# Loading the rows of x1 earlier, spreading the attention gates, and moving one absolute value in a fused two-layer convolution kernel

## The chip, the cores and the metric

The kernel runs on one core of a Trainium2 chip. The metric is the device time of one execution in microseconds. Kernels are compared by the median of their executions. The profile is of one execution. Engines carry the names of the profile: PE is TensorE (PEld its weight loads), DVE is VectorE, ACT is ScalarE, POOL is GpSimd, SP is SyncE, which here only issues transfers. DMAs are issued by SP, ACT and POOL.

## What is computed

The input is 32 images of 96 channels and 56 by 56 pixels, in float32. Two layers follow one another.

Layer 0 is an inverted bottleneck with squeeze and excitation. Its weights pass through `fake_quant` (8 bits).

```python
h = silu(bn(conv1x1(x, w1)))            # 96 -> 576 channels
h = silu(bn(depthwise3x3(h, w2)))
s = sigmoid(W2 @ silu(W1 @ mean(h) + b1) + b2)
x1 = x + bn(conv1x1(h * s, w3))         # 576 -> 96
```

Layer 1 attends x1 with a channel gate and a spatial gate, and then deforms it.

```python
mag = abs(rfft2(x1)); ca = channel_gate(mag)             # one number per channel
sa  = spatial_gate(mean(x1), l2(x1), resize(mean(mag)))  # one number per pixel
y = x1 * ca * sa
aux = concat(y, coordinates, resize(mean(abs(rfft2(y)))))
offset = conv3x3(aux)                   # 18 channels
gate = sigmoid(conv1x1(relu(conv3x3(aux))))
y_base = conv3x3(y)
y_def = deformed 3x3 convolution of y: 9 taps, each sampled bilinearly at its offset
z = (1 - gate) * y_base + gate * y_def
out = relu(batch_norm(z over all images and pixels) + x1)
```

## The kernel before, in words

`layers()` computes x1 and z of all images and stores them in DRAM; `normalise()` then reads both back and applies the batch norm. A branch for offsets that reach too far isn't taken with these inputs.

An image is cut into seven bands of eight rows. The main loop in `layers()` runs over the 224 bands of all images, and a band has two halves of seven tiles of 4 by 4 pixels for each of its two tile rows. Beside the sampling of band n of image b, three streams run ahead. They are Python generators, which issue a few instructions at each step and then yield. `pump()` advances them once per slot; an image has 70 slots, so one is about 4.2 us.

- `first` is `hidden()` of image b + 2: the expansion (L166 on PE, L170 on ACT), the depthwise taps (L257 and L259 on DVE), and SiLU (L219 on ACT) with the store to `h2d` on ACT's queue.
- `second` is `attend()` of image b + 1: the projection, whose operands `hq` come from `h2d` (L307 on SP, L323 on PE, L325 on ACT), with the residual added on POOL (L443) and x1 stored in DRAM (`x1d`, L444); then the magnitudes of the transform (`dft_mag`, x loaded by SP at L351, L376 to L400), the channel gate `ca`, the spatial gate `sa` (sigmoid L273 and L274), its store `sad` (L538 on POOL), and a second transform of x1 gated by sa (L356 on POOL), which gives the row `fq`.
- `find(n + 2)` is `offsets()` for the band two ahead, advanced once per slot within the band: the joint 3x3 convolution (L582 on PE), its hidden part (L603 on ACT), the offsets copied out of PSUM (`at`, L630, two on DVE), the base convolution (L606 and L614 on ACT, L611 on PE, L616 on DVE), the offsets to DRAM (`od`, L634 on POOL's queue) and back, spread over partitions (`ht`, L646 on SP). Then come the bilinear weights 1 - |offset - position|: the absolute value (Abs, L649) and Relu (L650), both on ACT, and a store to DRAM (`hd`, L653 on ACT's queue).

For each half band, `prepare()` loads column and row weights from hd (`wc` and `wr`, L664 and L665 on SP, four loads of 252 KB) and `weights()` multiplies them (L671 on DVE). `block_channels()` copies the pixels out (L682 on POOL), transposes them (L686 on PE, L688 on ACT), `sample_tiles()` multiplies them with the weights (L700 on PE, copied out by L704 on ACT to `v`), `pack()` moves channels onto the free partitions (L711, three on ACT), and `deform()` runs the deformed convolution (`pd`, L719 on PE). `gate_of()` gives the gate (L727, L729), `combine()` z (L745 to L748 on DVE).

The padded image of y, `yp`, is one buffer in SBUF whose rows are overwritten for the next image when the sampling of this one has left them. `refill(b, upto)` does that after each band: `load_rows()` loads x1 rows into it (L561 on SP) and the matching rows of sa, repeated over the channels, into `sab` (L563 on POOL's queue), and four slots later `attend_rows()` multiplies in place by ca and sab (L569 on DVE). It starts with the first call after sa exists. `load_freq()` puts the row fq in place (L573 on SP).

The list `later` holds actions that are due at a slot. At band 5 of an image (`turn`) the streams are drained, `flush()` runs everything in `later` at once, and the streams start anew for the next image.

What sets the order: SP is in a region whose schedule is manual, so it issues in the order in which the program was written. On the other engines a scheduler orders the instructions within their dependences. Pools with several buffers decide how far a load can run ahead; `hq` has eight, and an x1 group of seven rows needs five or six of them.

Of the kernel before, what the change touches and what calls it, by code (L numbers as in the profile page):

```python
# [9 lines left out]
AF = mybir.ActivationFunctionType  # L10
ALU = mybir.AluOpType
AX = mybir.AxisListType
PSUM = bass.MemoryType.PSUM
DRAM = bass.MemoryType.DRAM
# [6 lines left out]
RB = 8  # L21
# [277 lines left out]
def project_loads(nc, p, x, h2d, q):  # L299

    half, n0 = divmod(q * EW, HB)
    terms = [(u, ch, slice(0, 128)) for u, (ch, hf) in enumerate(UNITS) if hf == half]
    terms.append((4, 4, slice(64 * half, 64 * half + 64)))
    rows = []
    for u, ch, ps in terms:
        hq = p["hq"].tile([128, EW], FP, name="hq")
        nc.sync.dma_start(hq[ps], h2d[u, ps, n0 : n0 + EW])  # L307
        rows.append((ch, ps, hq))
    return rows
# [113 lines left out]
def attend(tc, p, b, x, h2d, pooled, x1, given=False):  # L423
# [5 lines left out]
    nc = tc.nc  # L429
    w = p["w"]  # L430
    if not given:
        rows = [project_loads(nc, p, x, h2d, 0)]
        yield from squeeze(nc, p, pooled)
        rows.append(project_loads(nc, p, x, h2d, 1))
        for _ in range(2):
            yield
        for q in range(H // ER):
            xr = residual_load(nc, p, x, q)
            o = project(nc, p, rows.pop(0))
            yield  # L440
            if q + 2 < H // ER:
                rows.append(project_loads(nc, p, x, h2d, q + 2))
            nc.gpsimd.tensor_tensor(o, o, xr, ALU.add)  # L443
            nc.gpsimd.dma_start(x1[:, q * EW : (q + 1) * EW], o)  # L444
            yield
    yield


# [43 lines left out]
    ca = p["ca"].tile([C, 1], FP, name="ca")  # L492
# [28 lines left out]
    r = p["sp"].tile([H, 3, W], FP, name="r")  # L521
# [5 lines left out]
    sa = p["sp"].tile([H, W], FP, name="sa")  # L527
# [6 lines left out]
    sa = p["sp"].tile([2 * H, W], FP, name="sa2")  # L534
# [20 lines left out]
    p["fq", b] = fqd  # L555


def load_rows(nc, p, yp, b, x1, r0, r1):

    rows = yp[:C, PD + r0 : PD + r1, PD : PD + W]  # L560
    nc.sync.dma_start(rows, x1.rearrange("c (h w) -> c h w", h=H)[:, r0:r1])  # L561
    sab = p["q2"].tile([C, RB, W], FP, name="sab")[:, : r1 - r0]
    nc.gpsimd.dma_start(sab, p["sa", b].rearrange("o (h w) -> o h w", h=H)[:, r0:r1].to_broadcast([C, r1 - r0, W]))  # L563
    return rows, sab


def attend_rows(nc, p, b, rows, sab):

    nc.vector.scalar_tensor_tensor(rows, rows, p["ca", b], sab, ALU.mult, ALU.mult)  # L569


def load_freq(nc, p, yp, b, r0, r1):
    nc.sync.dma_start(yp[CA - 1 : CA, PD + r0 : PD + r1, PD : PD + W], p["fq", b][:, r0:r1])  # L573
# [45 lines left out]
def offsets(nc, p, yp, j, top, hids, ybs, hds):  # L619

    w = p["w"]
    joint = joint_conv(nc, p, yp, j)
    hid, yb, pa = next(joint)
    hids.append(hid)
    ybs.append(yb)
    at = p["off"].tile([NOFF, NTX, 2, TP], FP, name="at")
    for s in range(2):
        nc.vector.tensor_copy(at[:, :, s].rearrange("o t (r c) -> o t r c", r=TS),  # L630
                              pa[:, s * BW // 2 : (s + 1) * BW // 2].rearrange("o (r t c) -> o t r c", r=TS, t=NTX))
    yield
    od = p["dp"].tile([NTX, 2, NOFF, TP], FP, name="od")
    nc.gpsimd.dma_start(od.rearrange("t s o p -> o (t s) p"), at.rearrange("o t s p -> o (t s) p"))  # L634
    yield
    next(joint)
    yield
    next(joint)
    yield
    next(joint, None)  # L640
    nc.vector.tensor_reduce(top, at.rearrange("o t s p -> o (t s p)"), AX.X, ALU.max, apply_absolute_value=True)
    for _ in range(4):
        yield
    ht = p["ht"].tile([SB * NTX, 4, KP], FP, name="ht")
    src = od.rearrange("t s o p -> t (s o p)").unsqueeze(0).to_broadcast([SB, NTX, 4 * KP])
    nc.sync.dma_start(ht.rearrange("q n k -> q (n k)"), src)  # L646
    for _ in range(4):
        yield
    nc.scalar.activation(ht, ht, AF.Abs, bias=w["blk"])  # L649
    nc.scalar.activation(ht, ht, AF.Relu, bias=w["one"], scale=-1.0)  # L650
    yield
    hd = p["dp"].tile([4, SB, NTX, KP], FP, name="hd")
    nc.scalar.dma_start(hd.rearrange("x i t n -> (i t) x n"), ht)  # L653
    hds.append(hd)
# [237 lines left out]
def pools(tc, ctx, p, space, sizes):  # L892
    for name, bufs in sizes:
        kw = {"space": space} if space else {}
        p[name] = ctx.enter_context(tc.tile_pool(name=f"l1{name}", bufs=bufs, **kw))


def layers(tc, a, dp, x1d, zd, stats, far):
# [6 lines left out]
    nc = tc.nc  # L905
    B = x1d.shape[0]
    with ExitStack() as ctx:
        p = {"dp": ctx.enter_context(tc.tile_pool(name="l1d", bufs=3, space=DRAM))}
        pools(tc, ctx, p, PSUM, (("mm", 6), ("acc", 1), ("pd", 1)))
        hidden_constants(tc, ctx, a, p)  # L910
        constants(tc, ctx, a, p)
        yp, = padded(nc, p, a, 1)
        top = p["cp"].tile([NOFF, NBD + 1], FP, name="top")
        nc.gpsimd.memset(top, 0.0)
        pools(tc, ctx, p, None, (("xt", 2), ("acch", 2), ("pl", 2), ("w3s", 1), ("hq", 8), ("o", 2), ("x2", 3),
                                 ("ca", 2), ("s1p", 1), ("xc", 2), ("sp", 1), ("sq", 1), ("q1", 2), ("q2", 2), ("hid", 3), ("yb", 4),
                                 ("off", 1), ("st", 2), ("ht", 1), ("wc", READY + AHEAD + 1), ("wr", AHEAD + 1), ("yt", 2), ("ybl", 1),
                                 ("vp", 2)))
# [15 lines left out]
        streams, later = [], []  # L934
        slot = 0

        def flush():
            while later:
                later.pop(0)[1]()
# [27 lines left out]
        def start(b, length):  # L967
            streams[:] = [[second(b + 1), 0, n_second, slot + 3, slot + length - 8],
                          [first(b + 2), 0, n_first, slot, slot + length]]
# [15 lines left out]
                for _ in st[0]:  # L985
                    pass

        filled = {}

        def refill(b, upto):  # L990

            upto = min(H, upto)
            r = filled.get(("y", b), 0)
            while ("sa", b) in p and r < upto:
                r1 = min(upto, r + RB)
                args = load_rows(nc, p, yp, b, x1d[b], r, r1)
                later.append((slot + 4, lambda args=args: attend_rows(nc, p, b, *args)))
                r = filled["y", b] = r1
            r = filled.get(("fq", b), 0)
            if ("fq", b) in p and r < upto:  # L1000
                load_freq(nc, p, yp, b, r, upto)
                filled["fq", b] = upto
# [29 lines left out]
        bands = [(b, j) for b in range(B) for j in range(NBD)]  # L1032
        hids, ybs, hds, ready = [], [], [], []

        def find(n):
            return offsets(nc, p, yp, bands[n][1], top[:, n % NBD : n % NBD + 1], hids, ybs, hds)
# [24 lines left out]
        for n, (b, j) in enumerate(bands):  # L1061
            if j == 0:
                st = p["st"].tile([C, NBD, 6], FP, name="st")
            if j == turn:
                drain()
                refill(b + 1, j * RB - PD)
                flush()
                start(b + 1, slots)
            more = find(n + 2) if n + 2 < len(bands) else iter(())
            next(more, None)  # L1070
            for h in range(2):
                v = p["vp"].tile([128, NTAP, NTH, 2, TP], FP, name="v")
                prepare(2 * n + h + READY + AHEAD)
                s = ready.pop(0)
                yt = yts.pop(0)
                for i, group in enumerate(GROUPS):
                    sample_tiles(nc, p, yt, s, v, group)
                    for _ in range(group[0][0], group[-1][1]):
                        next(more, None)
                        pump()  # L1080
                    if i == 0:
                        for end in ends:
                            end()
                        ends.clear()
                        if h == 1 and n + 1 < len(bands):
                            yts.append(block_channels(nc, p, yp, bands[n + 1][1], 0))
                        ready.extend(weights(nc, *ws) for ws in loads[:1])
                        del loads[:1]
                        if h == 0:
                            yts.append(block_channels(nc, p, yp, j, 1))  # L1090
                pack(nc, v)
                if h == 0:
                    gate = gate_of(nc, p, hids[n])
                ends.append(lambda n=n, h=h, v=v, gate=gate, st=st: end_half(n, h, v, gate, st))
            for _ in more:
                pass
            pump()
            pump()
            pump()
            if b + 1 < B:  # L1100
                refill(b + 1, (j + 1) * RB - PD if j < NBD - 1 else H)
            if j == NBD - 1:
                nc.vector.tensor_reduce(top[:, NBD:], top, AX.X, ALU.max)
# [349 lines left out]
```

## Time and profile before

| | |
|---|---|
| median of three executions | 9928.33 us (9917.45 to 9945.53) |
| the profiled execution | 9938.35 us |
| its span in the profile | 9936.6 us |
| mean granted clock of PE, share of full | 0.933 |
| PE busy | 8753.8 us (88%) |
| DVE busy | 7220.3 us (73%) |
| ACT busy | 5346.3 us (54%) |
| POOL busy | 2785.4 us (28%) |
| ACT at L649 waiting for ht | 736.3 us, 186 times |
| DVE at L569 waiting for x1 rows | 409.8 us, 64 times |
| moved by DMA | 1485.53 MB, 150 GB/s on average |

The span is that of the profiled execution, from its first instruction to its last; a wait in the profile is time in which an engine stood, put down to what came last before it went on. Idle time of an engine that isn't the bottleneck costs nothing by itself. In a timeline a line reads: start in us, duration in us, engine, source line, operation, output and inputs with their sizes, how many instructions were joined, and in brackets how long the engine had been idle and what released it. Line numbers in the text are those of the kernel before.

### The profile page before, as it was taken

How to read it: one execution, taken by the hardware profiler on the slowest of the kernel's cores; microseconds unless marked ns; L12 is line 12 of the kernel's file. 1: busy time of each engine (PE TensorE's matmuls, PEld its weight loads, DVE VectorE, ACT ScalarE, POOL GpSimd, SP SyncE). 2: the span in 40 equal slices, each digit the busy share in tenths (PEclk: the TensorE clock that was granted, in tenths of full speed). 3: DMA queues.
4: the chain of work that ended last, by engine and by line, in shares of the span. 5: the costliest groups of instructions: out<-in, count | busy, mean ns of one | idle time of the engine just before them, and what ended most of it. 6: DMA issues, size and time to landing. Idle time of an engine off the chain costs nothing. (4 is left out here: it accounts for less than half of the span.)

```text
span 9936.6 us, 122378 instructions
## 1 busy us (share of the span) xinstructions
PE 8753.8 (88%) x43766; PEld 5029.2 (51%) x43766; DVE 7220.3 (73%) x6948; ACT 5346.3 (54%) x10262; POOL 2785.4 (28%) x2639
## 2 busy tenths in 40 slices
PE   6899999998999999999899989999999999999970
PEld 3455555555555555555555555555555555555550
DVE  6688777777777777877777877777777777778323
ACT  2355555555555555555555555555555555555443
POOL 1132323332322333232233233233323223322210
PEclk9899999999999999999999999999999999999985
DMA  3345555554555555555555555555545555545549
GB/s 93 108 134 144 147 148 151 149 139 132 148 148 150 152 150 134 148 143 150 153 147 146 140 142 149 151 146 148 143 134 149 148 151 152 148 132 145 129 142 418
DMA packets 1085588, 1485.53 MB, mean 150 GB/s; under 512 B 606670, under 2 KB 856222, under 8 KB 1072686
## 3 DMA queue, kind: packets, MB, share of 16 engines
q1 hardware_dynamic: 875011, 985.23, 38.2%
q10 hardware_dynamic: 153675, 329.79, 8.9%
q0 software_dynamic: 56288, 162.60, 6.7%
q8 instruction: 352, 5.77, 0.3%
q14 instruction: 262, 2.15, 0.1%
HBM read 1064.28 MB, written 412.65 MB: 149 GB/s over the span
## 5 line engine op out<-in xcount | busy, mean ns | idle before, releaser
L259 DVE SCALAR_TENSOR_TENSOR acch<-hp,w,acch 128x1512 f32<-128x1512 f32 (+1 forms) x2250 | 4231.6, 1881 | 34.6
L682 POOL COPY ybl<-yp 96x448 f32<-96x448 f32 x896 | 1201.2, 1367 | 2065.8 <-PE mm L686 2065.3
L719 PE MATMUL pd<-v,c_def 128*96 128x224 f32 (+1 forms) x6272 | 1491.5, 391 | 315.0 <-ACT v L711 175.1
L582 PE MATMUL mm<-yp,c_jointW 104*128 104x448 f32 x4032 | 1609.2, 550 | 3.5 <-DMA yp<-fqd 3.5
L719 PEld LDWEIGHTS pd<-v,c_def 128*96 128x96 f32 (+1 forms) x6272 | 1100.7, 181 | 644.0 <-ACT v L711 192.8
L700 PE MATMUL mm<-wc,yt 64*96 64x144 f32 x12544 | 1124.4, 296 | 90.6 <-DVE yb L616 43.9
L323 PE MATMUL mm<-hq,w3s 128*96 128x392 f32 (+1 forms) x2560 | 1038.2, 546 | 168.7 <-DMA hq<-h2d 160.5
L582 PEld LDWEIGHTS mm<-yp,c_jointW 104*128 104x128 f32 x4032 | 762.3, 191 | 761.5 <-issue 694.7
L166 PE MATMUL mm<-xt,w 96*128 96x392 f32 (+3 forms) x2688 | 1077.4, 536 | 46.0 <-issue 33.0
L704 ACT COPY v<-mm 96x288 f32<-96x288 f32 (+1 forms) x2688 | 1005.8, 440 | 152.6 <-PE mm L700 120.2
L700 PEld LDWEIGHTS mm<-wc,yt 64*96 64x96 f32 x12544 | 861.9, 160 | 400.9 <-issue 233.5
L170 ACT ACTIVATE hp<-mm,sh,inv 128x392 f32<-128x392 f32 (+2 forms) x1216 | 816.0, 673 | 221.0 <-PE mm L166 143.2
L611 PE MATMUL mm<-yp,c_base0W 96*64 96x448 f32 x4032 | 916.7, 551 | 0.0
L671 DVE TENSOR_TENSOR wc<-wc,wr 128x1008 f32<-128x1008 f32 x448 | 551.9, 1232 | 458.0 <-DMA wr<-hd 349.3
L219 ACT ACTIVATE acch<-acch,sh,inv 128x1568 f32<-128x1568 f32 x288 | 486.9, 1690 | 642.2 <-DVE acch L259 641.1
L711 ACT COPY v<-v 32x448 f32<-32x448 f32 x1344 | 755.3, 562 | 28.7
L323 PEld LDWEIGHTS mm<-hq,w3s 128*96 128x96 f32 (+1 forms) x2560 | 410.1, 175 | 705.3 <-issue 576.6
L634 POOL DMA_DIRECT2D od<-at x224 | 185.9, 830 | 2046.4 <-DVE at L630 1655.6
L443 POOL TENSOR_TENSOR o<-o,xc 96x392 f32<-96x392 f32 x256 | 395.1, 1543 | 958.4 <-ACT o L325 955.9
L397 PE MATMUL mm<-s,c_GV 112*112 112x464 f32 x1536 | 659.5, 571 | 4.5 <-ACT s L383 4.5
L688 ACT COPY yt<-mm 128x384 f32<-128x384 f32 (+1 forms) x896 | 347.3, 439 | 500.1 <-PE mm L686 484.2
L569 DVE SCALAR_TENSOR_TENSOR yp<-yp,ca,sab 96x448 f32<-96x448 f32 x255 | 157.2, 626 | 576.7 <-DMA yp<-x1d 409.8
(191 smaller groups left out, 9184.6 us busy)
## 6 DMA issues: line engine op xcount, KB each, us to landing
h2d<-acch ACTq DMA_DIRECT2D x288, 784.0 KB
wc<-hd SPq DMA_DIRECT2D x896, 252.0 KB
wr<-hd SPq DMA_DIRECT2D x896, 252.0 KB
hq<-h2d SPq DMA_DIRECT2D x1024, 196.0 KB
x<-x1d SPq DMA_DIRECT2D x768, 98.0 KB
ht<-od SPq DMA_DIRECT2D x224, 252.0 KB
hd<-ht ACTq DMA_DIRECT2D x224, 252.0 KB
xt<-in_x SPq DMA_DIRECT2D x64, 609.0 KB
```

Of the source, the lines that this page charges most:

```text
L166: nc.tensor.matmul(pt[p0 : p0 + w1.shape[1], : rows * W], w1, xts[hf][:, r0 * W : (r0 + rows) * W], start=True, stop=True)
L170: nc.scalar.activation(h1[lo:hi, row0 : row0 + rows, 1 : 1 + W], pt[lo:hi, : rows * W].rearrange("p (h w) -> p h w", h=rows), AF.Silu, bia ...
L259: nc.vector.scalar_tensor_tensor(acc[:, lo:hi], win, wk, acc[:, lo:hi], ALU.mult, ALU.add)
L323: nc.tensor.matmul(pt[:C, :EW], w3s[ps, ch], hq[ps], start=(i == 0), stop=(i == NCH - 1))
L397: nc.tensor.matmul(pt[: 2 * W, :n].rearrange("p (q u) -> p q u", q=NPB), w["GV"][:, g], m, start=(k == 0), stop=(k == 1))
L582: nc.tensor.matmul(view, weights[:, k], yp[:channels, r0 : r0 + RB, dx + PD - 1 : dx + PD - 1 + W], start=(k == 0), stop=(k == NTAP - 1))
L611: nc.tensor.matmul(pb[k % 2 * BC : (k % 2 + 1) * BC, :BW].rearrange("p (h w) -> p h w", h=RB), w["base"][:, k], yp[:C, r0 : r0 + RB, dx + ...
L682: nc.gpsimd.tensor_copy(yb[:, :, s], blocks)
L700: nc.tensor.matmul(pt[k][:C, (t - lo) * KP : (t - lo + 1) * KP], yt[ps, t], s[ps, t * KP : (t + 1) * KP], start=True, stop=True)
L704: nc.scalar.copy(v[:C, :, lo:hi, k].rearrange("c k t p -> c t k p"), pt[k][:C, : (hi - lo) * KP].rearrange("c (t k p) -> c t k p", t=hi - ...
L711: nc.scalar.copy(v[C:, 1 + 2 * i : 3 + 2 * i], v[i * QC : (i + 1) * QC, KA:])
L719: nc.tensor.matmul(out.rearrange("c q (t x) -> c t q x", x=TS), p["w"]["def"][ks, k], v[ks, k].rearrange("c t s (r x) -> c t (s r) x", r=T ...
```

## The change

Four edits are made together.

- Abs is issued six slots after the load of ht instead of four, and pinned: `keep_in_program_order` makes the scheduler keep it behind the instruction of ACT that was written just ahead of it.
- `hq` has nine buffers instead of eight.
- `load_rows()` is split. The x1 rows are loaded into yp from the time the last part of x1 was issued (a flag `p["x1", b]`); the rows of sa are loaded by `load_gate()` once sa exists, for all rows that have been loaded by then.
- The multiplications of a call to `refill()` are spread: the first is due at slot + 3, the next at slot + 4, and so on, each pinned in the order of DVE. `flush()` at the turn is gone; in its place `need()` runs, before the offsets of a band are sought, those multiplications whose rows the band touches.

```diff
@@ attend
             nc.gpsimd.dma_start(x1[:, q * EW : (q + 1) * EW], o)
             yield
+    p["x1", b] = True
     yield
@@ load_rows and attend_rows
-def load_rows(nc, p, yp, b, x1, r0, r1):
+def load_rows(nc, yp, x1, r0, r1):
     rows = yp[:C, PD + r0 : PD + r1, PD : PD + W]
     nc.sync.dma_start(rows, x1.rearrange("c (h w) -> c h w", h=H)[:, r0:r1])
+    return rows
+
+
+def load_gate(nc, p, b, r0, r1):
     sab = p["q2"].tile([C, RB, W], FP, name="sab")[:, : r1 - r0]
     nc.gpsimd.dma_start(sab, p["sa", b].rearrange("o (h w) -> o h w", h=H)[:, r0:r1].to_broadcast([C, r1 - r0, W]))
-    return rows, sab
+    return sab
...
-    nc.vector.scalar_tensor_tensor(rows, rows, p["ca", b], sab, ALU.mult, ALU.mult)
+    end = nc.vector.scalar_tensor_tensor(rows, rows, p["ca", b], sab, ALU.mult, ALU.mult)
+    p["tc"].keep_in_program_order(end)
@@ offsets
-    for _ in range(4):
+    for _ in range(6):
         yield
-    nc.scalar.activation(ht, ht, AF.Abs, bias=w["blk"])
+    p["tc"].keep_in_program_order(nc.scalar.activation(ht, ht, AF.Abs, bias=w["blk"]))
@@ layers
-("hq", 8)
+("hq", 9)
...
-        filled = {}
+        filled, loaded, pending = {}, [], []
+
+        def attended(end):
+            if end in pending:
+                pending.remove(end)
+                end[1]()
+
+        def need(upto):
+            for end in [e for e in pending if e[0] < upto]:
+                attended(end)

         def refill(b, upto):
             upto = min(H, upto)
-            r = filled.get(("y", b), 0)
-            while ("sa", b) in p and r < upto:
+            r = filled.get(("x", b), 0)
+            while ("x1", b) in p and r < upto:
                 r1 = min(upto, r + RB)
-                args = load_rows(nc, p, yp, b, x1d[b], r, r1)
-                later.append((slot + 4, lambda args=args: attend_rows(nc, p, b, *args)))
-                r = filled["y", b] = r1
+                loaded.append((b, r, r1, load_rows(nc, yp, x1d[b], r, r1)))
+                r = filled["x", b] = r1
+            wait = slot + 3
+            while ("sa", b) in p and loaded:
+                _, r, r1, rows = loaded.pop(0)
+                sab = load_gate(nc, p, b, r, r1)
+                end = [r, lambda rows=rows, sab=sab: attend_rows(nc, p, b, rows, sab)]
+                pending.append(end)
+                later.append((wait, lambda end=end: attended(end)))
+                wait += 1
...
             if j == turn:
                 drain()
                 refill(b + 1, j * RB - PD)
-                flush()
                 start(b + 1, slots)
+            if n + 2 < len(bands):
+                need(bands[n + 2][1] * RB + RB + 1)
             more = find(n + 2) if n + 2 < len(bands) else iter(())
```

More of the change, by code (lines that the diff above doesn't have):

```diff
@@ L907, in layers @@
     with ExitStack() as ctx:
-        p = {"dp": ctx.enter_context(tc.tile_pool(name="l1d", bufs=3, space=DRAM))}
+        p = {"tc": tc, "dp": ctx.enter_context(tc.tile_pool(name="l1d", bufs=3, space=DRAM))}
         pools(tc, ctx, p, PSUM, (("mm", 6), ("acc", 1), ("pd", 1)))
@@ L914, in layers @@
         nc.gpsimd.memset(top, 0.0)
-        pools(tc, ctx, p, None, (("xt", 2), ("acch", 2), ("pl", 2), ("w3s", 1), ("hq", 8), ("o", 2), ("x2", 3),
+        pools(tc, ctx, p, None, (("xt", 2), ("acch", 2), ("pl", 2), ("w3s", 1), ("hq", 9), ("o", 2), ("x2", 3),
                                  ("ca", 2), ("s1p", 1), ("xc", 2), ("sp", 1), ("sq", 1), ("q1", 2), ("q2", 2), ("hid", 3), ("yb", 4),
```

## The prediction

> **What bounds the kernel now.** I read the page's busy times and slices first, then TensorE's waits, then windows and the timeline around the longest gaps of one image, counted by line.
>
> ```profile
> PE 8753.8 (88%) x43766; PEld 5029.2 (51%) x43766; DVE 7220.3 (73%) x6948; ACT 5346.3 (54%) x10262; POOL 2785.4 (28%) x2639
> ```
>
> TensorE is the bound. Between 500 and 9,650 us it repeats one pattern every 292.7 us (one image, seven bands). What the change can win lies in its gaps. TensorE's waits (us in total, times, longest):
>
> ```profile
> PE pd L719 <- ACT v L711: 175.1, 36, 8.2
> PE mm L323 <- DMA hq<-h2d: 160.5, 66, 7.7
> PE pd L719 <- ACT v L704: 138.2, 35, 6.2
> PE mm L376 <- POOL x L356: 128.1, 34, 5.0
> ...
> PE mm L700 <- DVE yb L616: 43.9, 33, 5.4
> ```
>
> About one of each per image; L323 two. Counted from the timeline, an image has 24.3 us of gaps. By the band k whose offsets are being sought: k2 5.65 (pack L711), k6 4.73 (copies L704), k5 4.20 (x of L356) and 1.29 (L616), k1 3.96 and k0 1.23 (both hq), the rest 3.2.
>
> A gap also costs clock. Windows of 100 us (busy PE, PEld, DVE, ACT, POOL; granted clock; DMA share):
>
> ```profile
> 5800.00:5900.00 100.00, 97.12 (x523) 55.22 (x523) 83.79 (x88) 61.96 (x125) 29.47 (x22) 0.98 0.43 119
> 6000.00:6100.00 100.00, 85.69 (x390) 47.31 (x389) 65.66 (x62) 48.53 (x90) 26.67 (x31) 0.89 0.67 179
> ```
>
> Gaps of 4 to 6 us are followed by 6.8 us at half clock, those of 1.4 to 2.6 us by 3.4 us, those of 1.2 to 1.5 us in half of the cases: about 30 us per image. At k1 the projection waits for hq:
>
> ```profile
> 4582.56 0.78 ACT L649 ACTIVATE ht<-ht,c_blk 112x576 f32<-112x576 f32 x1 [4.90 <-DMA ht<-od]
> ...
> 4583.09 5.14 PE L323 MATMUL mm<-hq,w3s 128*96 128x392 f32 x10 [3.52 <-DMA hq<-h2d]
> ```
>
> At k2 and k6 ScalarE waits for ht, then runs Abs (L649) and Relu (L650) while the pack that the deformable product needs stands behind:
>
> ```profile
> 4620.84 0.78 ACT L649 ACTIVATE ht<-ht,c_blk 112x576 f32<-112x576 f32 x1 [0.78 <-DMA ht<-od]
> ...
> 4624.76 1.74 ACT L711 COPY v<-v 32x448 f32<-32x448 f32 x3
> ...
> 4625.38 0.81 PE L719 MATMUL pd<-v,c_def 128*96 128x224 f32 x3 [2.60 <-ACT v L711]
> ```
>
> ```profile
> 4781.97 0.78 ACT L649 ACTIVATE ht<-ht,c_blk 112x576 f32<-112x576 f32 x1 [2.13 <-DMA ht<-od]
> 4782.65 0.67 ACT L704 COPY v<-mm 96x288 f32<-96x288 f32 x2
> ...
> 4784.63 1.81 PE L719 MATMUL pd<-v,c_def 96*96 96x224 f32 x4 [3.72 <-ACT v L704]
> ```
>
> At k5, where sa is ready, VectorE stands at the first gate and L616 behind it holds TensorE:
>
> ```profile
> 4724.03 0.68 DVE L569 SCALAR_TENSOR_TENSOR yp<-yp,ca,sab 96x448 f32<-96x448 f32 x1 [4.66 <-issue]
> 4724.63 0.62 DVE L616 TENSOR_TENSOR yb<-yb,mm 64x448 f32<-64x448 f32 x1
> ...
> 4725.30 0.73 PE L700 MATMUL mm<-wc,yt 64*96 64x144 f32 x8 [1.31 <-DVE yb L616]
> ```
>
> [...]
>
> **The change, part by part.** No instruction is added or removed; orders differ, identically in each image. I read both instruction orders, engine by engine.
>
> *Ninth hq buffer.* A load of hq waits for L323 to free a buffer (SP at L307: 1,062.1 us, 439 times). With nine, the first load of the next group is issued about 18 us earlier, ahead of the four weight loads (252 KB each) behind which the two late groups land. At k0 that covers the whole 1.23 us: −1.2, and half the cases' 3.4 us at half clock (1.7 us lost): −0.9. At k1, 196 KB fewer are left of a queue that took 11 to 13 us from issue to use; I take 1.7 us of 3.96, and 3.4 instead of 6.8 us at half, worth 1.7 us, of which I count half since some falls into other waits: −0.9. Ends: 0 and −9.
>
> *Abs two slots later and pinned.* k0 and k5: no move. k1: one L170 and one L325 (0.67 + 0.67) come ahead, covered by the 4.90 us wait. k2: one L360 and one L383 (0.55 + 0.54) come ahead of Abs and run in its wait, so the pack stands 1.1 us earlier: −1.1, clock −0.2. k6: all four L704 (1.76) come ahead, and run from 4779.9 instead of 4782.65; the first products need only these; then Abs, one L711, L650 and two L711. The pack ends near 4785.2 instead of 4786.35: −1.1, and the gap is cut in two: clock −0.8. k3 and k4: Abs goes behind some 20 and 15 us of ScalarE work. There hd is later by as much; at k3 its store leaves at about 4674 instead of 4657. Queued behind it on SP is the weight load, which stood at 4667.1 and now waits until about 4679, with the next ht behind that; but this ht waits for od until 4683.9 anyway, and the weights are used at 4697. That is the cover, 18 us less some 12 of landing; gone, it would cost what the weights are late. Zero.
>
> *x1 rows early.* Three loads of SP (168 KB the largest, 462 in all) leave the place behind the six x loads at k4 for k2, k3 and k4. At k2 they stand ahead of two weight loads: the weight product L671 (VectorE) comes some 1.5 us later and at k3 stands ahead of two L400: +1.0 (0 to +1.5).
>
> *Gates spread and pinned.* Three places. At k1 the gates stand behind a depthwise pair instead of before it; the stall on VectorE shrinks from 10–11 us to about 7, and L630 at k2 comes some 3 us earlier: no credit, since ht lands by the queue. At k0, stall unchanged. At k5 the order L630, L630, L259, L641, L259, gate, L616 becomes L259 three times, gate, gate, L630, L630, L259, L616. The gate row lands 3.6 to 3.7 us after its issue, which follows the three L356 on GpSimd. Sa itself is about 1.6 us earlier, since on ScalarE its sigmoid is moved ahead of L170 and L219 (0.67 + 1.69). VectorE stalls about 7 us, now in front of L630; L606 waits for L630, and ScalarE with it, up to 9 us. The gap at L616 grows from 1.3 to 4–5 us, but the x gap of 4.20 that follows shrinks by as much, for L356 runs on during that time and starts 1.6 us sooner: 0, between −2.5 and +4.
>
> *L219 moved* ahead of the pack at k2 (1.69 + 0.19): hidden in ACT's idle time unless the depthwise is late: +0.3, between 0 and +1.9.
>
> Sum per image: −2.1 −2.6 −1.3 −1.9 +1.0 +0 +0.3 = −6.6 us. Over 31 images −205 us, against the profiled execution's 9,938.35 us (span 9,936.6). The final normalisation (some 270 us) is untouched. That execution is 10 us over the median shown, 9,928.33; from the median: 9,725 us.
>
> **The rivals.** (1) *The queue sets everything*: ht and hq land when the bytes ahead have moved, whatever the buffers; the ninth buffer shifts 196 KB from one crowded stretch to another. For it: the window at 6,000 us has a DMA share of 0.67; against it: 5,800 has 0.43. Then k0 and k1 gain nothing, k2 and k6 1.3 + 1.9, less 1.3, and half of it lost at k5: about −1 us per image, 9,900–9,930. (2) *The gates block the offsets* (the other side): at k5 the first gate row lands later than the cover. Cover is the 1.3 + 4.2 us that TensorE stands there already; the row landed at about 4724.0. If L606 is released more than 5.5 us after TensorE has run out, each us is one of the image's, and half clock follows. At 9 us of blocking that is 3.5 us, and some 2 to 3.5 more for 6.8 us at half clock; with the other gains halved (−3.3) the image is 2 to 4 us longer: 9,990–10,050. It decides from a loss of 3.3 us at k5 on. For it: L606's column of ScalarE work has L614, L170, L383 and L704 behind it; against: six mm banks, and the x gap's slack. (3) *All clock comes back*: gaps at k1, k2 and k6 all fall under the length that brings half clock, another 4 us: 9,600. (4) The pin orders nothing, the Abs staying where it was: excluded, since the built order shows the moves.
>
> **How the numbers follow.** Main forecast 0.55 (9,640–9,830), full clock 0.09, hidden 0.13, gates blocking 0.23. The range holds the main case, most of rival 3, rival 1 and part of rival 2: 9,610 to 9,980. 0.3% of the time is 30 us, about what a measurement of this kernel can tell from no change. Faster: 0.55 + 0.09 + a third of rival 1 = 0.69; same: 0.07; slower 0.24.
>
> **What would show it.** Right: TensorE's total on hq falls from 160.5 to under 80 us; on L704 from 138.2 to under 50; on L711 to 140; that on L356 falls while that on L616 rises; clock 0.93 to 0.945; VectorE's wait for yp of 409.8 shrinks. Wrong: hq's total unchanged (rival 1); a new TensorE wait of over 6 us per image at k5, on ScalarE's yb or on L616, and ACT's L606 wait far over 109.4 (rival 2).

## The result, and the profile after

The changed kernel takes 9,828.08 us (median; 9,807.4 to 9,852.77), the kernel before, on the same chip, 9,936.93 us. The ratio is 0.9892, with a 95% interval of 0.9861 to 0.9923. The forecast was 9,725 us from 9,928.33, with a range of 9,610 to 9,980: the direction and the range hold, and of the forecast gain of about 203 us some 109 came.

The change adds lines, so the line numbers behind L443 are larger in the changed kernel: L569 is L575 there, L603 is L610, L606 is L613, L616 is L623, L630 is L637, L649 is L656, L671 is L678, L688 is L695, L700 is L707, L704 is L711, L711 is L718 and L719 is L726. The text uses the numbers of the kernel before, and the blocks of profile lines those of the kernel they are from.

Busy times of the changed kernel in its profile (busy us, share of the span, instructions):

```profile
PE 8823.5 (90%) x43766; PEld 5053.7 (51%) x43766; DVE 7220.9 (73%) x6948; ACT 5367.5 (55%) x10262; POOL 2692.3 (27%) x2639
```

TensorE's busy time has risen by 69.7 us, and the mean granted clock is 0.935 instead of 0.933, where 0.945 was expected. TensorE's waits in the changed kernel (us in total, times, longest):

```profile
PE pd L726 <- ACT v L718: 194.6, 91, 5.4
PE mm L323 <- DMA hq<-h2d: 99.2, 48, 6.1
PE mm L707 <- ACT hp L170: 53.8, 51, 1.9
PE acc L416 <- DVE m_fe L413: 48.9, 32, 2.1
PE mm L166 <- ACT yt L695: 35.6, 24, 3.2
...
PE pd L726 <- ACT v L711: 16.7, 34, 1.9
...
PE mm L707 <- DVE yb L623: 13.2, 26, 2.2
PE mm L376 <- POOL x L356: 12.7, 23, 3.4
```

Three of the old waits nearly went: the one for L704 (138.2 to 16.7 us), for L356 (128.1 to 12.7), for L616 (43.9 to 13.2). That for hq fell from 160.5 to 99.2. The wait for the pack rose from 175.1 to 194.6, and in 91 pieces instead of 36. The waits for L170 and, at L166, for L688 were small before (6.0 and 5.8 us).

The bands show where the time went. The table gives the length of each band in us, from one L603 to the next, as mean over 24 images of the trace, with TensorE's idle time and its time at half clock (a granted clock of 0.5 in the trace) per image. The three columns on the right are experiments 1 to 3.

| band k | before | changed | nine buffers alone | absolute value alone | rows and gates alone |
|---|---|---|---|---|---|
| 0 | 38.6 | 37.5 | 38.1 | 38.2 | 38.5 |
| 1 | 50.0 | 48.8 | 48.8 | 50.4 | 50.1 |
| 2 | 44.6 | 43.0 | 41.6 | 42.7 | 41.9 |
| 3 | 39.7 | 42.9 | 39.4 | 44.6 | 42.8 |
| 4 | 35.4 | 34.5 | 35.4 | 34.3 | 34.5 |
| 5 | 47.7 | 46.8 | 47.7 | 45.6 | 47.7 |
| 6 | 36.8 | 35.4 | 36.7 | 35.1 | 36.0 |
| image | 292.7 | 289.0 | 287.8 | 291.0 | 291.5 |
| idle | 24.6 | 18.3 | 20.5 | 19.3 | 21.7 |
| at half clock | 30.2 | 28.2 | 25.2 | 28.7 | 30.2 |
| gaps over 1.3 us | 5.1 | 5.9 | 4.8 | 5.8 | 6.4 |

Six bands became shorter, by 7.0 us, and band 3 became 3.2 us longer. Idle time fell by 6.3 us, but in more and shorter gaps, and half clock fell by 2.0 us only. Band 3 had 0.1 us at half clock before and has 4.8 now. Its middle in the kernel before, in one image:

```profile
4658.25 0.64 DVE L400 TENSOR_TENSOR s<-sq 112x464 f32<-112x464 f32 x1 [0.17 <-ACT sq L399]
4659.05 1.21 DVE L671 TENSOR_TENSOR wc<-wc,wr 128x1008 f32<-128x1008 f32 x1 [0.16 <-DMA wr<-hd]
4662.09 0.64 DVE L400 TENSOR_TENSOR s<-sq 112x464 f32<-112x464 f32 x1 [1.83 <-ACT sq L399]
```

And in the changed kernel:

```profile
1708.11 0.64 DVE L400 TENSOR_TENSOR s<-sq 112x464 f32<-112x464 f32 x1 [1.13 <-ACT sq L399]
...
1717.91 1.21 DVE L678 TENSOR_TENSOR wc<-wc,wr 128x1008 f32<-128x1008 f32 x1 [8.05 <-DMA wr<-hd]
1719.04 0.64 DVE L400 TENSOR_TENSOR s<-sq 112x464 f32<-112x464 f32 x1
...
1719.77 1.00 ACT L399 ACTIVATE sq<-mm 112x464 f32<-112x464 f32 x2 [5.94 <-DVE s L400]
...
1725.35 0.93 PE L166 MATMUL mm<-xt,w 96*128 96x392 f32 x2 [2.03 <-ACT yt L695]
...
1728.18 0.55 PE L416 MATMUL acc<-c_RT,m_fe 112*29 112x112 f32 x2 [1.91 <-DVE m_fe L413]
```

VectorE stands 8.05 us at the weight product L671, whose weights are still being loaded, and the L400 behind it could have run. This image is one of the longer ones: over the 24 images the wait is 5.9 us on average, from 3.0 to 8.8, against 0.5 in the kernel before. ScalarE's L399 waits 5.94 us for that L400, the copies L688 come late, and TensorE has two gaps of 2 us where it had one of 0.9.

At k2 there is a second gap:

```profile
2543.13 1.69 ACT L219 ACTIVATE acch<-acch,sh,inv 128x1568 f32<-128x1568 f32 x1 [2.99 <-DVE acch L259]
...
2545.51 1.73 ACT L718 COPY v<-v 32x448 f32<-32x448 f32 x3
...
2546.12 1.43 PE L726 MATMUL pd<-v,c_def 128*96 128x224 f32 x3 [2.73 <-ACT v L718]
```

L219, now ahead of the pack, waits 2.99 us for the depthwise part, and TensorE 2.73 us for the pack. This is the longest case. Over the 24 images L219 waits 1.3 us on average, and TensorE's gap is 1.3 us on average, from nothing to 2.7, over 1.3 us in 13 images. And at k5 the gates stand ahead of the copies of the offsets:

```profile
2363.87 1.16 DVE L575 SCALAR_TENSOR_TENSOR yp<-yp,ca,sab 96x336 f32<-96x336 f32 x2 [4.22 <-DMA sab<-sad]
...
2365.06 0.69 DVE L637 COPY at<-mm 18x224 f32<-18x224 f32 x2
2365.78 0.63 ACT L613 ACTIVATE yb<-mm,c_cvec 32x448 f32<-32x448 f32 x1 [7.53 <-DVE at L637]
...
2366.46 0.48 PE L707 MATMUL mm<-wc,yt 64*96 64x144 f32 x2 [0.33 <-ACT yb L613]
```

ScalarE is held for 7.53 us. TensorE has small gaps there, 2.7 us in the band instead of 5.5.

### The profile page after: what moved, and what is told of

It is laid out like the page before. It is cut to its first block, busy times and chain, and to the rows that moved or that the text cites. A ratio compares the mean times of both kernels' runs of the same rounds, so it can differ in the third digit from the quotient of the medians.

```text
span 9828.9 us, 122530 instructions
## 1 busy us (share of the span) xinstructions
PE 8823.5 (90%) x43766; PEld 5053.7 (51%) x43766; DVE 7220.9 (73%) x6948; ACT 5367.5 (55%) x10262; POOL 2692.3 (27%) x2639
## 3 DMA queue, kind: packets, MB, share of 16 engines
q1 hardware_dynamic: 875011, 985.23, 38.8%
## 5 line engine op out<-in xcount | busy, mean ns | idle before, releaser
L259 DVE SCALAR_TENSOR_TENSOR acch<-hp,w,acch 128x1512 f32<-128x1512 f32 (+1 forms) x2250 | 4270.2, 1898 | 34.5
L689 POOL COPY ybl<-yp 96x448 f32<-96x448 f32 x896 | 1147.5, 1307 | 2054.5 <-PE mm L693 2053.3
L589 PE MATMUL mm<-yp,c_jointW 104*128 104x448 f32 x4032 | 1648.1, 561 | 7.2 <-DMA yp<-fqd 3.4
L726 PE MATMUL pd<-v,c_def 128*96 128x224 f32 (+1 forms) x6272 | 1446.3, 380 | 219.1 <-ACT v L718 194.6
L726 PEld LDWEIGHTS pd<-v,c_def 128*96 128x96 f32 (+1 forms) x6272 | 1054.6, 175 | 538.5 <-ACT v L718 238.3
L707 PE MATMUL mm<-wc,yt 64*96 64x144 f32 x12544 | 1159.2, 301 | 131.2 <-ACT hp L170 53.8
L589 PEld LDWEIGHTS mm<-yp,c_jointW 104*128 104x128 f32 x4032 | 786.6, 197 | 801.0 <-issue 750.9
L166 PE MATMUL mm<-xt,w 96*128 96x392 f32 (+3 forms) x2688 | 1094.7, 544 | 69.5 <-ACT yt L695 35.6
L323 PE MATMUL mm<-hq,w3s 128*96 128x392 f32 (+1 forms) x2560 | 1025.7, 540 | 115.9 <-DMA hq<-h2d 99.2
L707 PEld LDWEIGHTS mm<-wc,yt 64*96 64x96 f32 x12544 | 879.4, 162 | 464.9 <-issue 234.3
L678 DVE TENSOR_TENSOR wc<-wc,wr 128x1008 f32<-128x1008 f32 x448 | 551.9, 1232 | 761.0 <-DMA wr<-hd 579.9
L711 ACT COPY v<-mm 96x288 f32<-96x288 f32 (+1 forms) x2688 | 1001.4, 441 | 170.7 <-PE mm L707 128.3
L170 ACT ACTIVATE hp<-mm,sh,inv 128x392 f32<-128x392 f32 (+2 forms) x1216 | 813.7, 671 | 234.7 <-PE mm L166 161.8
L219 ACT ACTIVATE acch<-acch,sh,inv 128x1568 f32<-128x1568 f32 x288 | 487.3, 1692 | 621.9 <-DVE acch L259 609.5
L718 ACT COPY v<-v 32x448 f32<-32x448 f32 x1344 | 755.2, 562 | 29.2
L443 POOL TENSOR_TENSOR o<-o,xc 96x392 f32<-96x392 f32 x256 | 405.1, 1582 | 997.8 <-ACT o L325 997.8
L166 PEld LDWEIGHTS mm<-xt,w 96*128 96x128 f32 (+1 forms) x2688 | 368.9, 182 | 473.5 <-issue 315.0
L695 ACT COPY yt<-mm 128x384 f32<-128x384 f32 (+1 forms) x896 | 350.8, 440 | 457.9 <-PE mm L693 454.6
```

Source lines behind the costliest of these rows:

```text
L166: nc.tensor.matmul(pt[p0 : p0 + w1.shape[1], : rows * W], w1, xts[hf][:, r0 * W : (r0 + rows) * W], start=True, stop=True)
L170: nc.scalar.activation(h1[lo:hi, row0 : row0 + rows, 1 : 1 + W], pt[lo:hi, : rows * W].rearrange("p (h w) -> p h w", h=rows), AF.Silu, bia ...
L259: nc.vector.scalar_tensor_tensor(acc[:, lo:hi], win, wk, acc[:, lo:hi], ALU.mult, ALU.add)
L323: nc.tensor.matmul(pt[:C, :EW], w3s[ps, ch], hq[ps], start=(i == 0), stop=(i == NCH - 1))
L589: nc.tensor.matmul(view, weights[:, k], yp[:channels, r0 : r0 + RB, dx + PD - 1 : dx + PD - 1 + W], start=(k == 0), stop=(k == NTAP - 1))
L689: nc.gpsimd.tensor_copy(yb[:, :, s], blocks)
```

## Experiments

Each ratio is to the kernel before on the same chip.

### 1 to 3: each part alone

```diff
-("hq", 8)
+("hq", 9)
```

> The kernel before with one edit of four: nine hq buffers. Theory A (each edit acts in its own bands): the gaps at k0 and k1 shrink as in the changed kernel, TensorE waits about 100 us for hq instead of 160.5, band k0 is 1.1 and band k1 1.2 us shorter: -2.3 us per image, some -70 us, ratio 0.993. Rival B (the load queue sets the landing): the waits only move, ratio 0.999 to 1.001. Band k3 stays at 39.7 us in both.

Measured: 9,799.35 us, ratio 0.987 (0.9842 to 0.9897). One number in one line gives as much as the whole change; the two intervals overlap. TensorE's waits:

```profile
PE pd L719 <- ACT v L704: 145.4, 34, 7.0
PE mm L376 <- POOL x L356: 129.3, 33, 4.8
PE mm L323 <- DMA hq<-h2d: 99.4, 58, 5.8
PE pd L719 <- ACT v L711: 97.0, 36, 6.7
```

The wait for hq is that of the changed kernel, as theory A has it, and L704 and L356 are untouched. What neither theory had: the wait for the pack L711 falls from 175.1 to 97.0. The orders on TensorE, GpSimd and SP are those of before, on VectorE three L671 per image and on ScalarE two pairs of L649 and L650 move by one to three places, none of them at k2. Abs at k2 starts 24.7 us after L603 instead of 27.7 (medians over the 24 images); it still waits for its ht, whose load SP issues after 15.2 us instead of 16.8. Ahead of that load SP issues the six x loads and four weight loads. The first x load leaves after 9.6 us instead of 11.3, just behind the landing of the last part of x1 (9.4 instead of 11.1), which the projection makes. So the buffer lets the projection end sooner, and ht follows; this is how the trace reads, and no run isolates that path. Of the 5.0 us per image 3.0 are at k2.

The absolute value alone:

```diff
-    for _ in range(4):
+    for _ in range(6):
         yield
-    nc.scalar.activation(ht, ht, AF.Abs, bias=w["blk"])
+    p["tc"].keep_in_program_order(nc.scalar.activation(ht, ht, AF.Abs, bias=w["blk"]))
```

> The kernel before with the absolute value two slots later and pinned, nothing else. Theory A: k2 and k6 are 1.6 and 1.4 us shorter, the rest stays, some -90 us, ratio 0.991. Rival C (the late store of hd at k3 makes the weights late and is the cause of the new gaps at k3): band k3 is 42 to 43 us here instead of 39.7, and the gain is cancelled, ratio about 1.000.

Measured: 9,891.21 us, ratio 0.9963 (0.9949 to 0.9977). k2 and k6 are 1.9 and 1.7 us shorter, k4 and k5 1.1 and 2.1 us as well, but k3 is 4.9 us longer. Early x1 rows, which this kernel hasn't, are not needed for the loss at k3. Whether the late hd is its cause, as rival C says, is for experiments 5 and 6.

Rows and gates alone, that is the changed kernel with eight buffers and

```diff
-    for _ in range(6):
+    for _ in range(4):
         yield
-    p["tc"].keep_in_program_order(nc.scalar.activation(ht, ht, AF.Abs, bias=w["blk"]))
+    nc.scalar.activation(ht, ht, AF.Abs, bias=w["blk"])
```

> The kernel before with the third and fourth edit: x1 rows early, gates spread and pinned; eight hq buffers, the absolute value as before. Theory A (the early x1 rows stand ahead of the weight loads, so the product L671 waits on VectorE ahead of two L400 and k3 gets two gaps and a piece at half clock): k3 is 3 us longer, k5 about 1 to 2 us shorter, +30 to +60 us in sum, ratio 1.003 to 1.006. Rival C (the absolute value is the cause at k3): k3 stays at 39.7 us, ratio 0.994 to 0.997.

Measured: 9,912.03 us, ratio 0.9984 (0.9969 to 0.9998). k3 is 3.1 us longer, but k2 is 2.7 us shorter and k5 isn't shorter at all. The moved absolute value isn't needed for the loss at k3 either.

The three ratios multiply to 0.982; together they give 0.9892. The parts don't add: each alone shortens k2, by 3.0, 1.9 and 2.7 us, all together by 1.6; and two of them lengthen k3. At k2 each takes from the same wait of TensorE for the pack, 5.7 us per image before: it is 3.2, 1.2 and 3.5 us in the three.

### 4: x1 rows as late as before

```diff
-            while ("x1", b) in p and r < upto:
+            while ("sa", b) in p and r < upto:
```

> The changed kernel, but with the x1 rows loaded only once sa exists, as before; the gates stay spread and pinned. Theory A: band k3 goes back from 42.9 to about 39.7 us, its half clock from 4.8 to under 0.5 us, some -100 us against the changed kernel: 9,730 us, ratio 0.979 to the kernel before. Rival C: k3 stays at 42.9 us, time 9,830. Rival D (the early rows are what shortens k5, since the gates don't wait for rows any more): k3 falls, but k5 rises by 2 to 3 us from 46.8, and the time stays within 30 us of the changed kernel's.

Measured: 9,788.94 us, ratio 0.9854 (0.9823 to 0.9886), k3 41.9 us with 4.1 us at half clock, k5 46.9. None of the three as stated: the rows are a part of the loss at k3 (1.0 of 3.2 us), not all of it, and the early load isn't what shortened k5.

In the built orders the kernels with the loss at k3 had one thing in common: on VectorE the weight product L671 stands ahead of the last two L400 of the magnitude, and in the kernel before and that with nine buffers alone it stands ahead of the last one only.

### 5: the weight product kept in program order

```diff
-    nc.vector.tensor_tensor(wc, wc, wr, ALU.mult)
+    tc.keep_in_program_order(nc.vector.tensor_tensor(wc, wc, wr, ALU.mult))
```

> The changed kernel with one more pin: the weight product L671 stays in program order on VectorE in every band, so that at k3 it follows the L400s instead of standing ahead of the last two. Theory E (the loss at k3 is this order: VectorE waits there for the weights that are still being loaded, while L400 could run): band k3 goes from 42.9 to about 39.7 us with under 0.5 us of half clock; -3.2 us per image, 9,730 us, ratio 0.980. Rival A (the early x1 rows are the cause, through the queue): k3 falls by no more than 1 us, 9,800 or more.

Measured: 9,752.92 us, ratio 0.984 (0.9803 to 0.9877). k3 is 39.2 us, with 0.3 us at half clock; theory E holds there. Band 3 in this kernel:

```profile
2288.16 0.64 DVE L400 TENSOR_TENSOR s<-sq 112x464 f32<-112x464 f32 x1 [4.41 <-ACT sq L399]
2290.63 1.20 DVE L678 TENSOR_TENSOR wc<-wc,wr 128x1008 f32<-128x1008 f32 x1
...
2296.21 0.35 PE L416 MATMUL acc<-c_RT,m_fe 112*29 112x112 f32 x2 [1.24 <-DVE m_fe L413]
```

The product runs without a wait, and the gap at L166 is gone. The rows were early and the absolute value late in this kernel too; so it is through the order on VectorE that both cost time at k3. The pin works in all bands, though, and k4 to k6 are 1.0, 0.4 and 0.5 us longer than in the changed kernel, with 5.3 us of gaps at L376 in k5.

### 6: the absolute value moved in bands 4 to 6 only

```diff
-    for _ in range(6):
+    for _ in range(6 if j >= 4 else 4):
         yield
-    p["tc"].keep_in_program_order(nc.scalar.activation(ht, ht, AF.Abs, bias=w["blk"]))
+    end = nc.scalar.activation(ht, ht, AF.Abs, bias=w["blk"])
+    if j >= 4:
+        p["tc"].keep_in_program_order(end)
```

> The changed kernel with its absolute value moved and pinned only for the bands 4, 5 and 6; bands 0 to 3 as before. On ScalarE L219 then stands behind the pack L711 at k2 again; on VectorE L671 at k3 stays ahead of the two L400. Theory F (L219 waiting for the depthwise ahead of the pack makes the gap at +17.5 us of band k2): that gap of 2.2 to 2.7 us is gone, k2 falls from 43.0 to about 41.6 us, k3 stays at 42.9: -45 us, 9,785, ratio 0.985. Rival C (hd is late at k3, and that is what costs there): k3 falls to 39.7 us as well and the time to about 9,690.

Measured: 9,763.16 us, ratio 0.9847 (0.9812 to 0.9881). L219 stands behind the pack again, TensorE's gap at that pack is gone in all 24 images, and k2 is 41.9 us, as theory F says. k3 stays at 42.7 us although hd leaves 16.8 us after L603 instead of 35.9: the late hd isn't needed for the loss, and rival C falls for the changed kernel. In experiment 2, where hd was late and the rows were not early, it can have added to the wait.

### 7 and 8: two combinations

Nine buffers and that edit, without the row and gate edits:

> The kernel before with nine hq buffers and the absolute value moved and pinned in bands 4, 5 and 6 alone; rows and gates as before. If bands add up: -5.0 us per image from the buffers and -4.8 from k4 to k6 (as the absolute value alone gave there: 35.4 to 34.3, 47.7 to 45.6, 36.7 to 35.1), k3 stays at 39.5: 283 us per image, 9,630 us, ratio 0.970. If the gains of k5 came from elsewhere: 9,720 to 9,760.

Measured: 9,660.62 us, ratio 0.9762 (0.9718 to 0.9806). k4 35.3, k5 45.5, k6 34.2 us, k3 39.7: k5 adds up as expected (45.6), k6 is better (35.1 expected), and k4 gains nothing (34.3 expected). Its ratio is below that of the changed kernel, and the intervals don't overlap.

The changed kernel with the edits of 5 and 6 together:

> The changed kernel with both mends: the absolute value moved only in bands 4 to 6, and the weight product pinned. Theories E and F together: k2 41.6, k3 39.7 us, -4.6 us per image, 9,685 us, ratio 0.975. If the spread gates cost more at k5 than the old ones with the absolute value moved there, k5 stays at 46.8 us and this kernel is slower than the one without the row and gate edits.

Measured: 9,751.39 us, ratio 0.9841 (0.9806 to 0.9877). k2 and k3 are 41.4 and 40.0 us, as expected, but k5 and k6 47.2 and 35.8, and the kernel is slower than that of experiment 7, as the last sentence has it. As in experiment 5, k5 has 5.4 us of gaps at L376 with the pin in all bands.

### 9: gates told apart by image

Why do the gates stand ahead of L630 at k5, if their multiplications are spread? `need()` compares row numbers only. The pending gates belong to the next image and have rows 0 to 22, and when the offsets of band 5 of this image are sought, `upto` is 49: all are forced at once.

```diff
-                end = [r, lambda rows=rows, sab=sab: attend_rows(nc, p, b, rows, sab)]
+                end = [b * H + r, lambda rows=rows, sab=sab: attend_rows(nc, p, b, rows, sab)]
...
-                need(bands[n + 2][1] * RB + RB + 1)
+                need(bands[n + 2][0] * H + bands[n + 2][1] * RB + RB + 1)
```

> The changed kernel, with the function that forces pending gates told apart by image. In the changed kernel it compares row numbers alone, so the gates of the next image are all forced before the offsets of band 5 of this one are sought, and their spreading is void: they stand ahead of L630 on VectorE. Here they stand behind L630. Theory H (this order holds L606 and with it TensorE at k5): ScalarE's wait of L606 for L630 falls from 254 to about 110 us, k5 from 46.8 to 45.5 and k6 from 35.4 to 34.3 us: -2.4 us per image, 9,755 us, ratio 0.983. Rival: what TensorE loses at k5 moves to the x of L356 again, k5 stays within 0.5 us and the time within 20 us of the changed kernel's.

Measured: 9,814.63 us, ratio 0.9889 (0.9866 to 0.9912). L630 stands ahead of the gates, and ScalarE's wait of L606 is 111.4 us in total instead of 254.3. But k5 and k6 are 46.4 and 34.9 us, and TensorE waits for x again:

```profile
PE mm L376 <- POOL x L356: 100.7, 35, 3.4
```

The rival holds: the same band has two waits in a row, for L606 and for x, and time saved at the first is lost at the second. So ScalarE's 142.9 us of further waiting at L606 in the changed kernel looked bad and cost next to nothing, 13 us of the whole time.

### 10: three mends of the changed kernel

The edits of 6 and 9, and the pin of 5 on one product per image instead of all:

```diff
-                        ready.extend(weights(nc, *ws) for ws in loads[:1])
+                        ready.extend(weights(nc, *ws, *([tc] if j == 2 and h == 0 else [])) for ws in loads[:1])
```

> The changed kernel with three mends: the absolute value moved in bands 4 to 6 alone, one weight product per image (first half of band 2) pinned behind the L400s, gates forced by image. If all three theories hold and add: -1.4 (k2), -3.2 (k3), -2.4 (k5, k6): 282 us per image, 9,610 us, ratio 0.969, 50 us below the kernel with only the buffers and bands 4 to 6. If early rows and spread gates are worth nothing once mended: 9,640 to 9,680, the same as that kernel. If early rows still delay the weights: k3 above 41 us and 9,700 or more.

Measured: 9,635.15 us, ratio 0.9714 (0.9688 to 0.974). k3 is 39.3 us and k5 45.7, which is 1.2 us less than in experiment 6; which of the two other mends does that isn't separated. The interval overlaps that of experiment 7, so the row and gate edits, once mended, are not shown to be worth anything.

### 11: the absolute value behind the pack at k2

To experiment 7, with the single pin of 10:

```diff
-    for _ in range(6 if j >= 4 else 4):
+    for _ in range({2: 7, 4: 6, 5: 6, 6: 6}.get(j, 4)):
         yield
     end = nc.scalar.activation(ht, ht, AF.Abs, bias=w["blk"])
-    if j >= 4:
+    if j >= 4 or j == 2:
```

> The kernel with nine buffers and the absolute value moved in bands 4 to 6, and in band 2 by seven slots, so that it stands behind the pack there; the weight product of the first half of band 2 is pinned. Theory G (at k2 the pack is late only because Abs waits for ht ahead of it): the gap of 3.1 us there goes, half clock at k2 from 4.0 to under 1 us, k2 from 41.1 to 37 to 38 us, 9,540 us, ratio 0.964. Rival: hd of band 2 leaves some 6 us later, the weights of its first half land later, and L700 or L671 waits at k3 instead: k3 2 to 4 us longer, time within 40 us of 9,660.

Measured: 9,519.65 us, ratio 0.96 (0.9572 to 0.9628), the fastest of all. Theory G holds. At k2 (L715 is the pack here, L723 the deformable product):

```profile
2486.73 1.73 ACT L715 COPY v<-v 32x448 f32<-32x448 f32 x3
2487.35 2.51 PE L723 MATMUL pd<-v,c_def 128*96 128x224 f32 x12 [0.39 <-ACT v L715]
...
2488.49 0.78 ACT L649 ACTIVATE ht<-ht,c_blk 112x576 f32<-112x576 f32 x1
```

The pack runs ahead of Abs, the gap is 0.39 us, k2 is 38.2 us with no half clock, and k3 40.0 instead of 39.7: the later hd of band 2 costs little there.

### 12: idle products in the gaps

To test the price of the half clock by itself, products with a zero weight were added to experiment 7 in two of TensorE's gaps. They add zero to what `pd` holds.

```diff
                          start=(k == 0), stop=(k == KA - 1))
+        for _ in range({0: 6, 4: 5}.get(j, 0) if h and k == 0 else 0):
+            nc.tensor.matmul(out.rearrange("c q (t x) -> c t q x", x=TS), p["zero"], v[:C, 0].rearrange("c t s (r x) -> c t (s r) x", r=TS),
+                             start=False, stop=False)
```

> The kernel with nine buffers and the absolute value moved in bands 4 to 6, with idle products added on TensorE: in the second half of bands 0 and 4, between the first tap of the deformable product and the second, which waits for the pack, 12 and 10 products with a zero weight are accumulated (about 2.4 and 2.0 us of the gaps at k2 and k6). The orders of ScalarE and VectorE stay as they were. Theory K [...]: half clock at k2 and k6 falls from 4.0 and 4.4 to under 1.5 us each, -2.5 to -3 us per image, 9,575 us, ratio 0.967. Rival: the clock falls anyway, or the products only lengthen the chain: half clock unchanged and 9,660 to 9,690.

Measured: 9,682.08 us, ratio 0.9757 (0.9736 to 0.9777), no faster than experiment 7. Half clock at k2 and k6 does fall, from 4.0 and 4.4 to 1.6 and 0.9 us, near what theory K forecast, but the time is that of the rival. k2 is 41.0 us instead of 41.1 and k6 34.7 instead of 34.2, and over the whole image half clock is 15.5 instead of 16.9 us, since k0, k1 and k5 have more. (The trace of experiment 7 is of an execution of 9,634 us and this one of 9,709, so differences of the bands of some tenths of a us mean little.)

Where did the time go? The products that do work did become faster: in the same numbers, the deformable product takes 7.8 instead of 8.4 us at k2, and 9.5 instead of 10.7 at k6. At k2 TensorE has no gap from the end of its wait for the pack to the next L603, and this stretch is 10.7 instead of 11.6 us. The band's busy time at half clock is 1.3 instead of 3.1 us, so the 0.9 us gained is half of the difference. But what comes ahead became longer. Two waits of experiment 7 (us in total, times, longest):

```profile
PE pd L721 <- ACT v L713: 167.7, 77, 7.1
ACT ht L649 <- DMA ht<-od: 486.7, 139, 7.8
```

And of this kernel:

```profile
PE pd L721 <- ACT v L713: 77.7, 80, 5.6
ACT ht L649 <- DMA ht<-od: 596.5, 157, 8.0
```

At k2 TensorE still waits 1.6 us for the pack after the idle products, so these, 2.6 us, don't hold it up. But the wait ends 30.3 us after L603 instead of 29.5, mainly because ScalarE waits longer for ht (1.8 instead of 1.2 us) ahead of the pack. So what the clock gave was lost at the landing of ht. Why ht doesn't come sooner when TensorE is faster was not tested.

## Why the prediction was right, and where its steps failed

**The bound.** "TensorE is the bound" was read from the shares of the whole span. By band it is less clear. VectorE's busy share in the kernel before is 0.56 and 0.57 in bands 0 and 1, but 0.88, 0.81, 0.96, 0.80 and 0.81 in bands 2 to 6, where TensorE has 0.87, 0.96, 0.98, 0.88 and 0.87. At k2 and k4 the two are level. VectorE has little slack at k3 either (0.81): its wait of 5.9 us at L671 was passed on to TensorE, whose idle time there rose from 1.4 to 3.2 us, and this is how the change lost.

**Gaps.** The sum without its clock terms was −3.8 us of gaps per image, with k5 at nothing. Measured is −6.3. k0 came as forecast (1.23 to 0.2). k1 gave 1.1 of the forecast 1.7 us on hq, and 0.4 of these came back as a wait behind Abs; the total on hq, forecast under 80, is 99.2. k6 went as described: the first products need only L704, and that wait is 16.7 us, forecast under 50. The pack follows with 2.5 us per image. k5 was better than nothing, 2.8 us less idle, and the band 0.9 us shorter: the gap at x went (4.2 to 0.1 us per image), and the gap at L616, which was to grow, shrank (1.3 to 0.3), since TensorE's small waits on L170 and L606 (1.9 and 0.4 us) took its place.

**Clock.** The step "3.4 instead of 6.8 us at half … worth 1.7" failed, and the other clock terms with it: −2.8 us per image were forecast. TensorE's busy time per image rose by 2.6 us, from 268.1 to 270.7, of which the part run at half clock grew by 2.7 us, from 22.2 to 24.9, worth 1.4. The other 1.2 us the trace doesn't explain. The price of half the length isn't what was wrong: at k2 of experiment 12, 1.8 us less of busy time at half clock came with a stretch 0.9 us shorter. Wrong was that a shorter gap brings a shorter piece. Take the gaps of 1.5 to 2.6 us in 24 images that have no other gap over 0.8 us within 8 us. In the kernel before there are 10: 6 were followed by 3.4 us at half clock and 4 by none. In the changed kernel there are 55: 21 were followed by 6.8 us, 18 by 3.4 and 16 by none. (And of all gaps of 1.2 to 1.5 us in the kernel before it was 4 of 20, not half.) Gaps became shorter but more, 5.9 over 1.3 us instead of 5.1. TensorE's busy time, of which the clock explains a part, makes 5.4 us of the difference between −6.6 and the measured −3.7 us per image, against the gaps' 2.5 us that were better. That 9,828 us lies inside the range, and just inside the main forecast, is thus in part luck: two errors of opposite sign.

**k3.** The step "stands ahead of two L400: +1.0 (0 to +1.5)" named the mechanism and the place; the size was off, it is +3.2. I priced the product as 1.5 us late, and that is nearly what it is: it starts 22.6 us after L603 instead of 21.4 (means of 24 images). But its place in the order now comes up 5.9 us before its weights are there, and the two L400 wait behind it. How long depends on the landing of the offsets' store, behind which SP issues ht, then 168 KB of x1 rows, then the weights: where the store landed within 6.4 us of L603 (four images), the product waits 3.0 to 3.6 us and k3 takes 38.8 us, as short as in the kernel before; where it took 9 us or more (seven images), the wait is 6.9 to 8.8 us and k3 44.4 to 47.1. The store lands no later than before on average (7.9 us, 8.4 before). Experiment 5 takes 3.7 us out of k3 by the order alone, as the single pin of experiment 10 does (39.3 us). The late hd, which I had costed at zero with its cover, is worth 0.2 us between the changed kernel and experiment 6.

**k2.** "L219 moved ahead of the pack: +0.3, between 0 and +1.9" had the right mechanism and too small a middle. The gap it makes is 1.3 us on average, within the ends, because the wait of L219 for VectorE (1.3 us on average, up to 2.99) counts and not only its own 1.88. Taking the move back, together with the moved Abs, shortens k2 by 1.1 us (experiment 6), where the two were forecast to gain 1.0. The move comes from the absolute value's edit: it stands in the order of experiment 2 as well. There L219 waits 1.8 us and TensorE has no gap at that pack, so the order alone doesn't make the gap; what else it takes is open. Part of k2's loss was covered by the earlier ht, the gain of the ninth buffer that I had not seen, 3.0 us alone.

**Ninth buffer.** I gave it −4.7 us per image, of which 1.8 us clock. Alone it gives 5.0 in the trace and a ratio of 0.987. That the sum is right is luck in part: more than half of it is at k2, not at k0 and k1.

**Rivals.** Rival 1 (the queue sets everything) falls with experiment 1. Rival 2 (gates block the offsets) had the right wait: L606, which reads partitions 96 to 127 of a bank of which L630 reads 64 to 81, waited for L630 for 109.4 us in 67 cases before, and 254.3 us now. TensorE's own wait for L606 is 1.8 us at the longest, far from the 5.5 us beyond which it was to decide, and experiment 9 shows the rest: freed, the time is lost at x. Rival 3 (all clock comes back) falls with the 28.2 us at half clock.

**The signs.** As forecast: L704 under 50 us, less wait at L356, VectorE's wait for the rows of yp from 409.8 to 113.8 us. Not as forecast: hq at 99.2 instead of under 80, the pack L711 at 194.6 instead of 140, L616 falling instead of rising, the clock at 0.935 instead of 0.945.

## What to carry to other kernels

Where a scheduler sets the order, look up every pair that an edit swaps and ask what the instruction that is now in front waits for: its own duration is not its price (L671 takes 1.2 us, and in band 3 it waited 5.9). Read the busy shares by stage before you name the bound, and where two engines are level, count the stalls of both. A gain on one engine reaches the total only if the next wait in the same stage doesn't take it back: in experiment 9 ScalarE's wait for L630 fell by 142.9 us and the time by 13. And try each part of a compound change alone: here one buffer gave as much as all four parts.

## What the runs showed that was not expected

- With 12 and 10 small products per image (0.2 us each) in two of TensorE's gaps, its half clock at k2 and k6 fell from 4.0 and 4.4 to 1.6 and 0.9 us. The deformable product there became 0.6 and 1.2 us faster, but neither band more than 0.1 us shorter, and 4.1 us more at half clock appeared in k0, k1 and k5 together.
- With a ninth buffer in one pool another transfer came sooner, ht at k2 (its load issued 15.2 instead of 16.8 us after L603), and k2 became 3.0 us shorter, more than what the buffer did for its own consumer at k0 and k1 (1.7 us).
- With the same order in every image, band 3 of the changed kernel takes 38.8 to 47.1 us, depending on whether the store of the offsets lands 4.7 or 10.0 us after L603.
